# Gathering the first edge tiles from x while the normalized table is made

## The chip, the cores and the metric

The kernel runs on one core of a Trainium2 chip. The metric is the device time of one execution in microseconds, as a median over several runs; lower is better. Engines are named as in the profile: PE is TensorE, DVE is VectorE, ACT is ScalarE, POOL is GpSimd, SP is SyncE (here it only issues transfers).

## The reference

A layer of a graph network is followed by a mixture of experts, in fp32. There are 12500 nodes with 256 features and 212500 edges, sorted by their destination.

```python
f = layernorm(x)                                     # no learned scale
agg = segment_sum(f[src] * edge_weight[:, None], dst, 12500)
x = x + agg @ W.T + b
h = layernorm(x)
e = argmax(softmax(h @ gate_w + gate_b))             # one of 8 experts a token
y = relu(h @ w1[e] + b1[e]) @ w2[e] + b2[e]          # at most 1954 tokens an expert
x = x + nan_to_num(y * probability of e)
```

## The kernel before

**The table.** The first stage normalizes all rows of x and writes them to a table in device memory, `feat`. It runs over LCH: twelve chunks of eight tiles of 128 rows, then one of one tile, then a tail of 84 rows. For each chunk SP loads the rows (`xt`), DVE makes mean and variance (`ln_stats`: L171 and L172), ACT takes one square root for the chunk (L179), DVE inverts and refines it (L182 to L187) and scales the eight tiles (`ln_apply`, L198), and ACT issues the store to `feat` (L161). Two buffers of each kind let a load run ahead.

In the same stage DVE prepares the edges' places: `dst` becomes float, `rel` (the place of each edge's destination in a window of its group), `win` and, for a count of edges that break the windows (`n_bad`), seven more passes over all 1661 columns.

**The main loop.** The edges are cut into KT = 1661 tiles of 128. A loop written out by hand counts steps `s` from 0. In each step one edge tile is gathered, an older one is multiplied, and the other work moves on by one yield:

- `gather(s)` (L628): POOL issues an indirect DMA of 128 rows of `feat` by the indices `src_i[:, s]` into one of 32 buffers `m`.
- `onehot(k + 8)` (L636): DVE makes a weighted one-hot matrix, one of 12 buffers `h`. Here k = s - LEAD and LEAD is 16.
- `product(k)` (L645): PE multiplies it with the gathered rows. Fifteen tiles (a group) add up in one PSUM bank, and ACT copies the sum out (`ws`, L648).
- `fill`: one of 13 writes of 2.57 MB by SP (L223), which preset the pages `buf` of the experts' tokens.
- `nodes()`: for each node tile, the rows of x are loaded on ACT's queue (L669), PE shifts the sums of two to four groups into place (L681), ACT copies (L685), PE multiplies with W (L690), DVE adds x (L693) and makes statistics. After each chunk of eight tiles `ffn.route` normalizes, chooses the expert, and puts the tokens into `buf` (L318, POOL).
- `experts()`: pages of one expert's tokens are loaded, multiplied (L453, L464), finished on DVE and scattered to the output (L495, POOL). Constants count their pace in steps.

Each engine takes its instructions in this written order. A gather waits only for its buffer, so POOL can run up to 32 tiles ahead of the products. A node tile of 128 nodes takes 17 edge tiles. After the last edge tile the rest of the experts follows.

The first gather needs all of `feat`; the stage boundary gives up the first stage's buffers.

Of the kernel before, what the change touches and what calls it, by code (L numbers as in the profile page):

```python
# [9 lines left out]
F32 = mybir.dt.float32  # L10
I32 = mybir.dt.int32
U8 = mybir.dt.uint8
AF = mybir.ActivationFunctionType
ALU = mybir.AluOpType
# [40 lines left out]
AHEAD = 8  # L55
LOADED = 20
PACE = {1: 2.3, 2: 3.0}

# [25 lines left out]
def gnn_moe_kernel(ctx: ExitStack, tc: tile.TileContext, x, src, dst, ew, wT, gb, gate_w, gate_b,  # L86
# [69 lines left out]
    def load_rows(t, src_rows, t0, nt, rows, eng):  # L156
        eng.dma_start(t[:rows, :nt, :],
                      src_rows[t0 * P:t0 * P + nt * rows, :].rearrange("(j p) d -> p j d", p=rows))

    def store_rows(dst_rows, t, t0, nt, rows, eng):  # L160
        return eng.dma_start(  # L161
            dst_rows[t0 * P:t0 * P + nt * rows, :].rearrange("(j p) d -> p j d", p=rows),
            t[:rows, :nt, :])

    def ln_new(pool):
        return pool.tile([P, CH, 6], F32, name="bn"), pool.tile([P, CH, 2], F32, name="mv")

    def ln_stats(ln, x_, j, rows):  # L170
        nc.vector.bn_stats(ln[0][:rows, j, :], x_)  # L171
        nc.vector.bn_aggr(ln[1][:rows, j, :], ln[0][:rows, j, :])  # L172

    def ln_scale(pool, ln, nt, rows):
        v = pool.tile([P, CH], F32, name="ve")
        nc.vector.tensor_scalar_add(v[:rows, :nt], ln[1][:rows, :nt, 1], EPS)
        yield
        s = pool.tile([P, CH], F32, name="sd")
        nc.scalar.activation(s[:rows, :nt], v[:rows, :nt], AF.Sqrt)  # L179
        yield  # L180
        r = pool.tile([P, CH], F32, name="rs")
        nc.vector.reciprocal(r[:rows, :nt], s[:rows, :nt])  # L182
        q = pool.tile([P, CH], F32, name="rq")
        nc.vector.tensor_mul(q[:rows, :nt], r[:rows, :nt], r[:rows, :nt])
        nc.vector.tensor_mul(q[:rows, :nt], q[:rows, :nt], v[:rows, :nt])
        nc.vector.tensor_scalar(q[:rows, :nt], q[:rows, :nt], -0.5, 1.5, op0=ALU.mult, op1=ALU.add)
        nc.vector.tensor_mul(r[:rows, :nt], r[:rows, :nt], q[:rows, :nt])  # L187
        return r

    def through(g):  # L190
        while True:
            try:
                next(g)
            except StopIteration as e:
                return e.value

    def ln_apply(xn, x_, ln, r, j, rows):
        nc.vector.tensor_scalar(xn, x_, ln[1][:rows, j, 0:1], r[:rows, j:j + 1], op0=ALU.subtract,  # L198
                                op1=ALU.mult)
# [345 lines left out]
    with tc.tile_pool(name="edges", bufs=1) as edges:  # L545
# [2 lines left out]
        rel = edges.tile([P, NG * J], F32, name="rel")  # L548
        win = edges.tile([P, NGR], F32, name="win")

        with tc.tile_pool(name="p1", bufs=2) as p1, tc.tile_pool(name="eprep", bufs=1) as ep, \
                tc.tile_pool(name="epsum", bufs=1, space=PSUM) as eps:
            dst_i = ep.tile([P, NG * J], I32, name="dst_i")
            loads = [(dst_i, dst), (src_i, src), (w_sb, ew)]


            for i, (t0, nt, rows) in enumerate(LCH):
                xt = p1.tile([P, CH, D], F32, name="xt")
                load_rows(xt, x, t0, nt, rows, nc.sync)
                if i in (2, 3, 4):  # L560
                    to_sb, of = loads[i - 2]
                    nc.sync.dma_start(to_sb, of.rearrange("p g j -> p (g j)"))
                xn = p1.tile([P, CH, D], F32, name="xn")
                ln = ln_new(p1)
                for j in range(nt):
                    ln_stats(ln, xt[:rows, j, :], j, rows)
                r = through(ln_scale(p1, ln, nt, rows))
                for j in range(nt):
                    ln_apply(xn[:rows, j, :], xt[:rows, j, :], ln, r, j, rows)
                store_rows(feat, xn, t0, nt, rows, nc.scalar)  # L570


            dst_f = ep.tile([P, NG * J], F32, name="dst_f")
            nc.vector.tensor_copy(dst_f, dst_i)
            pb = eps.tile([P, NGR], F32, name="pb")
            nc.tensor.matmul(pb, ones[0:1, :], dst_f[0:1, 0:KT:G], start=True, stop=True)
            base = ep.tile([P, NGR], F32, name="base")
            nc.scalar.copy(base, pb)
            nc.vector.tensor_scalar(win, base, pcol, None, op0=ALU.add)
            line = ep.tile([P, NGR], F32, name="line")  # L580
            nc.gpsimd.iota(line, pattern=[[1, NGR]], base=0, channel_multiplier=0,
                           allow_small_or_imprecise_dtypes=True)
            nc.vector.tensor_scalar(line, line, SLOPE, None, op0=ALU.mult)
            off = ep.tile([P, NG * J], F32, name="off")
            whole = KT // G
            for t, of in ((rel, base), (off, line)):
                a = whole * G
                nc.vector.tensor_sub(t[:, :a].rearrange("p (g j) -> p g j", j=G),
                                     dst_f[:, :a].rearrange("p (g j) -> p g j", j=G),
                                     of[:, :whole, None].to_broadcast([P, whole, G]))  # L590
                if a < KT:
                    nc.vector.tensor_sub(t[:, a:KT], dst_f[:, a:KT],
                                         of[:, whole:whole + 1].to_broadcast([P, KT - a]))
            good = ep.tile([P, NG * J], F32, name="good")
            gv, rv, ov = good[:, :KT], rel[:, :KT], off[:, :KT]
            nc.vector.tensor_scalar(gv, rv, 0.0, None, op0=ALU.is_ge)
            nc.vector.scalar_tensor_tensor(gv, rv, float(P - 1), gv, op0=ALU.is_le, op1=ALU.mult)
            nc.vector.scalar_tensor_tensor(gv, ov, LOW + 0.05, gv, op0=ALU.is_ge, op1=ALU.mult)
            nc.vector.scalar_tensor_tensor(gv, ov, HIGH - 0.05, gv, op0=ALU.is_le, op1=ALU.mult)
            cnt = ep.tile([P, 1], F32, name="cnt")  # L600
            nc.vector.tensor_reduce(cnt, gv, axis=AX.X, op=ALU.add)
            pc = eps.tile([1, 1], F32, name="pc")
            nc.tensor.matmul(pc, ones[:, 0:1], cnt, start=True, stop=True)
            nc.vector.tensor_scalar(n_bad, pc, -1.0, float(P * KT), op0=ALU.mult, op1=ALU.add)

        nc.sync.dma_start(wT_sb, wT.rearrange("(k p) o -> p k o", p=P))
        nc.sync.dma_start(gb_sb, gb.partition_broadcast(P))
        nc.sync.dma_start(gw_sb, gate_w.rearrange("(k p) e -> p k e", p=P))
        nc.sync.dma_start(gateb_sb, gate_b.partition_broadcast(P))

        with tc.tile_pool(name="p2", bufs=32) as p2, tc.tile_pool(name="p2h", bufs=12) as p2h, \
# [11 lines left out]
            def gather(k):  # L626
                m = p2.tile([P, D], F32, name="m")
                nc.gpsimd.indirect_dma_start(  # L628
                    out=m, out_offset=None, in_=feat[:, :],
                    in_offset=bass.IndirectOffsetOnAxis(ap=src_i[:, k:k + 1], axis=0))  # L630
                ffn.before = None
                ms[k] = m

            def onehot(k):
                h = p2h.tile([P, P], F32, name="h")
                nc.vector.tensor_scalar(h, cols, rel[:, k:k + 1], w_sb[:, k:k + 1], op0=ALU.is_equal,  # L636
                                        op1=ALU.mult)
                hs[k] = h
# [81 lines left out]
                            outs.append(ffn.out)  # L720
                    yield

            now, outs = [0], []
            a, b = nodes(), None
            fill = ffn.fill()
            alive = True
            while alive or pages or b or outs:
                s = now[0]
                if s < KT:
                    gather(s)  # L730
                if pool_q:
                    f, j = pool_q.pop(0)
                    f(j)
                else:
                    for o in outs[:1]:
                        if next(o, None) is None:
                            outs.remove(o)
                k = s - LEAD
                if s == 0:
                    for i in range(AHEAD):  # L740
                        onehot(i)
                if 0 <= k < KT:
                    if k + AHEAD < KT:
                        onehot(k + AHEAD)
                    product(k)
                next(fill, None)
                if alive and k >= 0:
                    alive = next(a, 0) is None
                if pages and not b:
                    b = experts(now)  # L750
                if b and next(b, 0) == 0:
                    b = None
                now[0] += 1
# [136 lines left out]
```

## Time and profile before

| | us |
|---|---|
| runs | 3639.66, 3646.94, 3649.23; median 3646.94 |
| profiled execution, its own time | 3609.87 |
| span of the profiled execution | 3607.7 |
| first gather issued (L628, POOL) | 123.86 |
| last gather issued | 3357.6 |
| busy PE / DVE / ACT / POOL | 2035.1 / 1115.3 / 392.2 / 1787.2 |
| mean granted clock of PE | 0.776 |

The profile is one execution of the program. Busy time is the time in which an engine was executing, idle time is put down to whatever ended it, and the DMA share is the mean busy share of the core's 16 DMA engines. Times in the timelines are microseconds from the span's start. A stage table gives, for a stretch of time, the busy time of each engine with its number of instructions. In the operand names, `m<-feat,src_i` is an instruction that writes m and reads feat and src_i.

### The profile page before, as it was taken

What the parts mean: (1) busy time and instruction counts of PE and PEld (TensorE: products, weight loads), DVE (VectorE), ACT (ScalarE), POOL (GpSimd) and SP (SyncE); (2) the same over time, 40 slices, a digit from 0 to 9 for tenths busy, and PEclk for the clock granted to TensorE, in tenths of its full rate; (3) what the DMA queues carried; (4) which work ended last, traced back from release to release, by engine and by line L of the source; (5) the groups of instructions that cost most, each with busy time, mean ns of one, the idle gap of its engine ahead of it and who ended that gap; (6) DMA issues with size and microseconds to landing.
All of it is one profiled execution on the core that took longest, in us unless ns stands there. A gap on an engine that the chain in (4) does not pass through costs nothing. (4 is left out here: it accounts for less than half of the span.)

```text
span 3607.7 us, 30637 instructions
## 1 busy us (share of the span) xinstructions
PE 2035.1 (56%) x9078; PEld 1685.2 (47%) x9078; DVE 1115.3 (31%) x4110; ACT 392.2 (11%) x991; POOL 1787.2 (50%) x1860
## 2 busy tenths in 40 slices
PE   0335536475475475565565557555655646446865
PEld 0134435464364364354455446444444545345765
DVE  8422323232232232322323323222322323323422
ACT  0000000011011011011011011011110101001222
POOL 0466565644654645645545554554555464555200
PEclk9867767786787687787788778777777778678989
DMA  6865333532542533533433343343353252355665
GB/s 235 317 218 185 102 94 94 162 102 81 164 139 73 161 108 110 159 95 124 149 105 117 120 137 106 108 143 98 94 160 118 73 163 72 94 167 172 198 204 174
DMA packets 267818, 495.47 MB, mean 137 GB/s; under 512 B 45027, under 2 KB 162229, under 8 KB 267640
## 3 DMA queue, kind: packets, MB, share of 16 engines
q0 software_dynamic: 91920, 251.53, 22.6%
q1 hardware_dynamic: 136210, 203.42, 17.7%
q10 hardware_dynamic: 39510, 38.41, 3.3%
q8 instruction: 81, 1.33, 0.2%
q14 instruction: 97, 0.79, 0.1%
HBM read 399.69 MB, written 97.44 MB: 138 GB/s over the span
## 5 line engine op out<-in xcount | busy, mean ns | idle before, releaser
L628 POOL DMA_INDIRECT m<-feat,src_i x1661 | 1582.3, 953 | 816.1 <-issue 402.8
L645 PE MATMUL pw<-m,h 128*128 128x256 f32 x3322 | 1010.3, 432 | 250.8 <-DVE h L636 100.2
L645 PEld LDWEIGHTS pw<-m,h 128*128 128x128 f32 x3322 | 686.3, 219 | 386.2 <-issue 244.9
L636 DVE TENSOR_SCALAR h<-cols,rel,w_sb 128x128 f32<-128x128 f32 x1661 | 509.8, 359 | 767.2 <-remote 376.9
L453 PE MATMUL ph<-gT,w_sb 128*128 128x256 f32 (+1 forms) x1856 | 384.3, 360 | 255.9 <-issue 97.3
L453 PEld LDWEIGHTS ph<-gT,w_sb 128*128 128x128 f32 x1856 | 320.0, 208 | 301.6 <-issue 138.9
L495 POOL DMA_INDIRECT out<-z,tok x91 | 92.4, 1015 | 669.3 <-DVE h L636 444.5
L690 PE MATMUL ms<-wT_sb,aT 128*128 128x256 f32 x392 | 137.7, 485 | 445.8 <-ACT aT L685 315.4
L464 PE MATMUL py<-w_sb,hT 128*128 128x256 f32 x1456 | 374.3, 404 | 5.7 <-issue 4.5
L681 PE MATMUL ms<-s,ws 128*128 128x128 f32 x1116 | 197.7, 316 | 301.4 <-issue 196.8
L693 DVE TENSOR_TENSOR rt<-xt,ms 128x256 f32<-128x256 f32 x98 | 41.2, 420 | 1016.6 <-PE ms L690 593.3
L681 PEld LDWEIGHTS ms<-s,ws 128*128 128x128 f32 x1116 | 191.5, 228 | 324.0 <-issue 242.0
L464 PEld LDWEIGHTS py<-w_sb,hT 128*128 128x128 f32 x1456 | 296.5, 207 | 48.7 <-issue 3.7
L690 PEld LDWEIGHTS ms<-wT_sb,aT 128*128 128x128 f32 x392 | 87.9, 236 | 487.1 <-ACT aT L685 336.5
L318 POOL DMA_INDIRECT buf<-rt,to x98 | 111.2, 1135 | 320.4 <-DVE c L347 236.1
L457 ACT ACTIVATE hT<-ph,b_sb 128x256 f32<-128x256 f32 (+1 forms) x464 | 166.8, 426 | 803.8 <-remote 381.4
L256 PE MATMUL ms<-gw_sb,xT 128*128 128x8 f32 x392 | 70.4, 289 | 163.6 <-ACT xT L251 84.4
L256 PEld LDWEIGHTS ms<-gw_sb,xT 128*128 128x128 f32 x392 | 67.1, 239 | 200.3 <-ACT xT L251 118.4
L648 ACT COPY ws<-pw 128x256 f32<-128x256 f32 x111 | 41.2, 371 | 781.5 <-PE pw L645 383.5
L474 DVE TENSOR_TENSOR y<-py,b_sb 128x512 f32<-128x512 f32 (+1 forms) x58 | 33.4, 576 | 290.9 <-PE py L464 265.4
L258 DVE TENSOR_TENSOR lgs<-ms,gateb_sb 128x8 f32<-128x8 f32 x98 | 16.3, 167 | 288.9 <-PE ms L256 138.4
L685 ACT COPY aT<-ms 128x256 f32<-128x256 f32 x98 | 36.4, 372 | 636.1 <-remote 440.5
(143 smaller groups left out, 974.0 us busy)
## 6 DMA issues: line engine op xcount, KB each, us to landing
w_sb<-in_w SPq DMA_DIRECT2D x116, 1024.0 KB
buf<-fill SPq DMA_DIRECT2D x13, 2570.0 KB
m<-feat,src_i POOLq DMA_INDIRECT x1661
pg<-buf SPq DMA_DIRECT2D x33, 514.0 KB
xt<-in_x ACTq DMA_DIRECT2D x97, 128.0 KB
xt<-in_x SPq DMA_DIRECT2D x12, 1024.0 KB
feat<-xn ACTq DMA_DIRECT2D x12, 1024.0 KB
out<-rt ACTq DMA_DIRECT2D x11, 1024.0 KB
```

The costliest lines, as they stand in the source:

```text
L256: nc.tensor.matmul(pl[:rows, :], xT[:, k, :rows], gw_sb[:, k, :], start=(k == 0), stop=(k == 1))
L318: s = nc.gpsimd.indirect_dma_start(out=buf[:, :], out_offset=bass.IndirectOffsetOnAxis(ap=to[:, j, :], axis=0), in_=rt[:rows, j, :], in_of ...
L453: nc.tensor.matmul(ph[:, c:c + n], w1_sb[:, k, f * P:(f + 1) * P], xT[:, k * n:(k + 1) * n], start=(k == 0), stop=(k == 1))
L457: nc.scalar.activation(hT[:, f, :n], ph[:, c:c + n], AF.Relu, bias=b1_sb[:, f:f + 1])
L464: nc.tensor.matmul(py[:, a, :], hT[:, f, a * P:(a + 1) * P], w2_sb[:, f, :], start=(f == 0), stop=(f == F // P - 1))
L495: s = nc.gpsimd.indirect_dma_start(out=out[:, :], out_offset=bass.IndirectOffsetOnAxis(ap=to[:, a, :], axis=0), in_=z[:, a, :], in_offset= ...
L628: nc.gpsimd.indirect_dma_start(out=m, out_offset=None, in_=feat[:, :], in_offset=bass.IndirectOffsetOnAxis(ap=src_i[:, k:k + 1], axis=0))
L636: nc.vector.tensor_scalar(h, cols, rel[:, k:k + 1], w_sb[:, k:k + 1], op0=ALU.is_equal, op1=ALU.mult)
L645: nc.tensor.matmul(product.pw, hs.pop(k), ms.pop(k), start=(j == 0), stop=last)
L648: nc.scalar.copy(ws, product.pw)
L681: nc.tensor.matmul(pa[:, k * P:(k + 1) * P], sums[g][:, k * P:(k + 1) * P], shifts[t, g], start=(g == gs[0]), stop=(g == gs[-1]))
L690: nc.tensor.matmul(px[:rows, :], aT[:, k * P:k * P + rows], wT_sb[:, k, :], start=(k == 0), stop=(k == 1))
```

## The change

The table is no longer a stage of its own. A function `table()` runs inside the main block, before the loop, and does three things in one pass over the chunks:

- It gathers RB = 5 edge tiles in each of its 14 first passes, 70 in all, from `x` itself instead of `feat`. These rows are normalized in place: ACT sums each row (Identity with an accumulator output), a pass later sums the squares of the row minus its mean (Square with a bias and an accumulator output), and a pass after that scales them. The roots and inverses of the five tiles are taken together with those of the chunk's eight (B = 13 columns).
- Of a chunk's eight tiles, ACT scales six (Identity with bias and scale) and DVE two. The inverse of a chunk is taken one pass after its root.
- Four passes after their gather, the five tiles get their one-hots and products. 65 products are done in `table()`; the other five follow in the loop.

The loop then starts at step 70 with `done = made = 65`, and the node tiles may start at once; a product still comes LEAD steps after its gather, so the next one comes at step 81. The edges' places are made in pass 1 (`places()`), and the count `n_bad` is made in the loop's first steps, one DVE pass a step (`check()`). The index list is loaded first; the weights of the node tiles are loaded after the chunks. The buffers of the table are those of the experts' weights (three of each instead of two), which are not in use yet.

The diff, cut to its core:

```diff
+RB = 5
+RAW = RB * len(LCH)
...
             def gather(k):
...
-                    out=m, out_offset=None, in_=feat[:, :],
+                    out=m, out_offset=None, in_=x[:, :] if k < RAW else feat[:, :],
...
+            def table():
+                nc.sync.dma_start(src_i, src.rearrange("p g j -> p (g j)"))
...
+                for i in range(n + 3):
+                    if i < n:
+                        t0, nt, rows = LCH[i]
+                        xts[i] = p4.tile([P, CH, D], F32, name="xt", tag="w1_sb", bufs=3)
+                        load_rows(xts[i], x, t0, nt, rows, nc.sync)
+                        for k in range(i * RB, (i + 1) * RB):
+                            gather(k)
...
+                    if 0 <= i - 1 < n:
+                        batch[i - 1] = p3.tile([P, 2, RB], F32, name="sums", bufs=3)
+                        for j in range(RB):
+                            junk = p3.tile([P, D], F32, name="junk", bufs=1)
+                            nc.scalar.activation(junk, ms[(i - 1) * RB + j], AF.Identity,
+                                                 accum_out=batch[i - 1][:, 0, j:j + 1])
+                    if 0 <= i - 2 < n:
+                        sq[i - 2] = p3.tile([P, RB], F32, name="squares")
+                        for j in range(RB):
+                            junk = p3.tile([P, D], F32, name="junk", bufs=1)
+                            nc.scalar.activation(junk, ms[(i - 2) * RB + j], AF.Square,
+                                                 bias=batch[i - 2][:, 1, j:j + 1],
+                                                 accum_out=sq[i - 2][:, j:j + 1])
+                    if i >= 1:
+                        r = ln_inverse(p3, vs[i - 1], ss[i - 1], B, P)
...
+                        for j in range(nt):
+                            if j % 4 == 3:
+                                ln_apply(xn[:rows, j, :], xt[:rows, j, :], lns[i - 1], r, j, rows)
+                            else:
+                                nc.scalar.activation(xn[:rows, j, :], xt[:rows, j, :], AF.Identity,
+                                                     bias=nb[:rows, j:j + 1], scale=r[:rows, j:j + 1])
+                        store_rows(feat, xn, t0, nt, rows, nc.scalar)
+                    if 0 <= i - 3 < n:
+                        for j in range(RB):
+                            m = ms[(i - 3) * RB + j]
+                            nc.scalar.activation(m, m, AF.Identity, bias=nb[:, CH + j:CH + j + 1],
+                                                 scale=r[:, CH + j:CH + j + 1])
+                    if i == 1:
+                        places()
...
+                        for j in range(nt):
+                            ln_stats(lns[i], xts[i][:rows, j, :], j, rows)
...
+                    ss[i] = ln_root(p3, vs[i], B, P)
+                    if i >= 4:
+                        for k in range((i - 4) * RB, (i - 3) * RB):
+                            onehot(k)
+                            product(k)
...
-            now, outs = [0], []
+            done = table()
+            made = done
+            now, outs = [RAW], []
...
-            fill = ffn.fill()
+            extra = [ffn.fill(), check()]
...
-                k = s - LEAD
-                if s == 0:
-                    for i in range(AHEAD):
-                        onehot(i)
-                if 0 <= k < KT:
-                    if k + AHEAD < KT:
-                        onehot(k + AHEAD)
-                    product(k)
-                next(fill, None)
-                if alive and k >= 0:
+                while made < min(KT, max(done, s - LEAD) + AHEAD):
+                    onehot(made)
+                    made += 1
+                if done < KT and done <= s - LEAD:
+                    product(done)
+                    done += 1
+                for e in extra:
+                    next(e, None)
+                if alive:
```

## The prediction

> **What bounds the kernel now.** I read, in this order, the page, the stage table (busy time of each engine in stretches that I chose), the same table for the gathered tile m alone, the timelines of the table stage, and the ScalarE groups by form. The chain that ended last covers only the last scatter here and says nothing on the stages, so stages carry the argument. All engines by stretch, columns PE, PEld, DVE, ACT, POOL, clock, DMA share, GB/s:
>
> ```profile
> 0.00:123.80 123.80, 0.95 (x4) 0.58 (x4) 99.86 (x415) 4.35 (x16) 1.34 (x10) 1.00 0.69 234
> 123.80:221.00 97.20, 42.19 (x115) 24.95 (x116) 21.00 (x67) 1.49 (x4) 66.60 (x70) 0.72 0.82 297
> 414.00:3358.00 2944.00, 1717.89 (x7483) 1422.26 (x7482) 865.45 (x3129) 309.96 (x742) 1581.35 (x1636) 0.76 0.39 121
> ```
>
> The first 123.8 us make the table: VectorE is busy 81%, ScalarE 3.5%, POOL and TensorE do nothing. The next 97.2 us hold the first 70 gathers (POOL x70), so a gather costs 1.39 us there. In the long stage no engine is over 59%: the engines wait for each other along the written order of steps. Its 1471 gathers (m alone) make 2.00 us a gather, and nothing in the diff touches one of those steps. The two ends of the first 70 gathers, on POOL:
>
> ```profile
> 123.86 1.15 POOL L628 DMA_INDIRECT m<-feat,src_i  x1 [121.93 <-DVE h L636]
> ...
> 221.04 0.94 POOL L628 DMA_INDIRECT m<-feat,src_i  x1 [0.30 <-issue]
> ```
>
> The first waits 121.93 us for the table; the second is gather 70, the first that the changed kernel still takes from feat. How a chunk of the table runs (timeline):
>
> ```profile
> 90.07 2.67 DVE L198 TENSOR_SCALAR xn<-xt,mv,rs 128x256 f32<-128x256 f32 x8
> 92.72 0.75 DVE L171 BATCH_NORM_STATS2 bn<-xt 128x6 f32<-128x256 f32 x2
> 92.78 0.46 ACTq L161 DMA_DIRECT2D feat<-xn  x1
> ...
> 97.63 2.67 DVE L198 TENSOR_SCALAR xn<-xt,mv,rs 128x256 f32<-128x256 f32 x8
> ...
> 100.33 0.46 ACTq L161 DMA_DIRECT2D feat<-xn  x1
> ```
>
> A chunk takes 100.33 - 92.78 = 7.55 us, VectorE without a pause: 3.2 statistics, 1.7 the root and its inverse, 2.67 scaling.
>
> **What the skill says.** "ScalarE: Activation LUTs", What ACT_TABLE_LOAD costs: an ACTIVATE takes 186 ns + 0.833 ns an element, about 93 ns more for each per-partition pointer operand, and back-to-back ones overlap by 93 ns. The ScalarE groups agree:
>
> ```profile
> L477 ACT ACTIVATE y<-y,pg 128x256 f32<-128x256 f32 x91 | 42.6, 503 | 307.6 <-DVE y L474 242.7 <-issue 61.3 <-DMA w_sb<-in_w 3.6
> L179 ACT ACTIVATE sd<-ve 128x8 f32<-128x8 f32 x23 | 4.8, 209 | 128.4 <-DVE ve L176 113.4 <-issue 5.8 <-DVE h L636 2.9
> ```
>
> One pointer, 256 elements: the page's sum is 492, measured 503. "ScalarE activation tables: per-element evaluation and per-set limits", What a function is on this engine: the accumulator output adds results into the engine's accumulator. No price is given, and the kernel before has no such instruction. "DMA: Bandwidth & Descriptors", Queues, rings and completion order: each DMA engine goes round-robin between the queue rows with work. That fits 124 to 209 us, where fill writes and gathers share the engines (DMA share 0.85, 311 GB/s), POOL issues 62 gathers, but only 31 products (62 rows of m) run.
>
> **The change, part by part.**
>
> ScalarE in one full pass of the new table loop: five sums, no pointer, 399 - 93 = 306 ns by the page; five squares with a pointer bias, 492 - 93 = 399; six table scalings and five in-place scalings of m with two pointers, 585 - 93 = 492 each; the store's issue 0.46 (above); the root 0.21 and about 0.1 for its wait. The accumulator's read-out is unknown: no cost (lower bound) to one more small ACTIVATE plus the lost overlap, 0.209 + 0.093 = 0.30 us (upper). It can hardly be a gain, since work is added. I take 0.19. Sum: 5 x 0.50 + 5 x 0.59 + 11 x 0.49 + 0.77 = 11.6 us a pass; 9.7 and 12.7 at the bounds.
>
> Others in that pass: VectorE 3.2 statistics, 0.7 for two scalings, 1.3 inverse with its wait, 0.9 for five small ops, 1.5 for five one-hots = 7.6. POOL 5 x 1.25 (the steps of its timeline) = 6.3. DMA: 1.05 MB load, 1.05 store, 0.66 gathers = 2.75 MB, at the 281 GB/s of 60 to 100 us 9.8 us, at the 337 of 150 to 200 us 8.2. So ScalarE becomes the bound, with DMA close behind; that is why a free read-out buys little below 9.7. Square must not swap the table against Sqrt: a swap is 1.28 us by the ACT_TABLE_LOAD row. The page says cheap functions come in every set and gives square the budget of identity; I take none.
>
> The table's length: the source list now loads first, so the first root is at about 13 us (11.5 before). Pass 1 holds six scalings, and on VectorE the 4.2 us of places() (cast 1.0, rel 1.87, the matmul and copy between): to 24.5. Pass 2, 16 ACTIVATEs: to 34. Ten passes of 11.6: to 150. Pass 13, one table tile: 9.1, to 159. Pass 14 to its store: 6.5, to 165.7. Before, the last store's issue at 121.11 let the gather go at 123.86, 2.75 us later. Gather 70 starts at **168.5 us**, against 221.0: 52 us earlier. Passes 15 and 16 (8 us more on ScalarE) run beside it: POOL may be 32 buffers ahead of the products. The 65 products, 65 x 0.86 us, lie where TensorE was idle.
>
> What moves with it. The fills now begin at step 70 and slow gathers 70 to 140 as they slowed 0 to 70: both streams go through the same stretch, 70 gathers further on, so it cancels. Six VectorE passes of check() (10.4 us) move from a bound stage into steps 70 to 77, where no product is due before step 81: hidden. The three node loads that ScalarE issued early at 47 us, and the four weight loads from SP, now come at the table's end: 1.4 us of issue and a landing beside the fills, about 4 us, partly under the late gathers. I charge 4 in all: net **-48 us**.
>
> On the profiled execution's own time, 3609.87 (span 3607.7), this gives 3562; that execution lies 37 us under the median of the runs, 3646.94. The step is taken off the median: **3599 us**.
>
> **Rivals.**
>
> (1) Light ScalarE: the read-out is free, a pass is 9.7, DMA-bound too. Ten passes save 19 us more: gather 70 at 149.5, 3580. For it: the page has no price. Against: five results must leave an accumulator one by one.
>
> (2) Heavy ScalarE: each accumulating ACTIVATE must also wait for the one before (all write the same junk tile) and costs 0.35 above the 0.19. A pass is 15.1, gather 70 comes at 204, the gain is 17 - 4 = 13 us: 3634. At 17 us a pass it is gone.
>
> (3) Slower: the fills come too late for the first scatters. SP issued 13 fills over 193 us, and from 214 us on they follow the node loads (SP, then ScalarE's queue):
>
> ```profile
> 214.07 104.60 SPq L223 DMA_DIRECT2D buf<-fill  x6
> ```
> ```profile
> 211.86 0.37 ACTq L669 DMA_DIRECT2D xt<-in_x  x1
> 233.36 0.34 ACTq L669 DMA_DIRECT2D xt<-in_x  x1
> 254.86 0.33 ACTq L669 DMA_DIRECT2D xt<-in_x  x1
> ```
>
> The queues share completion semaphores, so fills wait for a load that comes once per node tile, 21.5 us apart. The last landed near 326 (318.3 and about 8); the first scatter into buf ran at 414.3 and waited for its own addresses. Shifted, the scatter is wanted at 414 - 52 = 362; the fills start 43 us later and end at 369. That is 7 us late at the old pace; but with node tiles 0 to 2 now ready at step 70 their loads come sooner, so I count none. If three more fills fall behind node loads, they end at 369 + 65 = 434: 72 us late, POOL stands on the scatter with all later gathers queued behind it, and 72 - 48 = 24 us are lost: 3671. It decides from two and a half more.
>
> (4) The change doesn't do what it says: the long stage gives back what the start won, because something not in the gather stream paces it. Against: groups of sums, node tiles and pages are all counted in gathers. No change, 3647.
>
> **How the numbers follow.** Forecast 0.62 (own range 3580 to 3618), rival 1 0.13, rival 2 0.12, rival 3 0.09, rival 4 0.04. A measurement of this kernel can tell about 0.3%, 11 us, from no change. Faster: 0.62 + 0.13 + most of rival 2 (0.10) = 0.85; same: 0.02 + 0.04 = 0.06; slower 0.09. The range runs from under rival 1 (3565) to past rival 2 (3638).
>
> **What would show it.** Right: ScalarE nearly full from 25 to 160 us, passes of 11 to 12 us between store issues, the first gather within 10 us of the start, gather 70 at 160 to 180, the long stage still at 2.0 us a gather. Wrong: store issues 9.7 apart (rival 1) or 14 and more (2); ACT_TABLE_LOADs in the table stage; a scatter into buf waiting for buf<-fill (3); more than 2.02 us a gather in the long stage (4).

## The result and the profile after

The changed kernel takes 3608.34 us, median of 5 runs (3603.12 to 3608.53), against 3646.94 for the kernel before (3632.55 to 3649.23) in the same comparison: 38.6 us less, a ratio of 0.990 with the 95% interval 0.988 to 0.9921. The forecast was 3599; its step of 48 us was 9 us too large. The profiled execution of the changed kernel is 3603.12 us, its span 3601.3, at a mean clock of 0.760.

The stage table of the changed kernel, cut at gather 70, at gather 140, and at the first put into `buf` and the last gather (columns PE, PEld, DVE, ACT, POOL, clock, DMA share, GB/s):

```profile
0.00:184.00 184.00, 47.34 (x108) 33.64 (x109) 97.64 (x443) 144.59 (x422) 69.56 (x79) 0.75 0.61 206
184.00:287.30 103.30, 55.17 (x194) 41.72 (x193) 41.55 (x125) 12.14 (x34) 72.28 (x71) 0.70 0.94 337
376.60:3348.50 2971.90, 1712.64 (x7483) 1425.45 (x7483) 858.09 (x3132) 310.42 (x741) 1578.96 (x1636) 0.75 0.40 120
```

In the table's stretch ScalarE is now the busiest engine, 144.59 of 184 us, where it had 4.35 of 123.8; POOL issues 70 gathers in it (x79 with its other work). The long stage holds the same 7483 matmuls and 1636 POOL instructions, and nearly the same busy times, as before. Its 1400 gathers from number 200 to 1600 take 2.00 us each (before: 1.99).

The two ends of the 70 raw gathers on POOL:

```profile
5.64 1.12 POOL L579 DMA_INDIRECT m<-in_x,src_i  x1 [3.90 <-DMA src_i<-in_src]
...
184.05 0.94 POOL L579 DMA_INDIRECT m<-feat,src_i  x1 [30.22 <-PE pw L596]
```

The first gather now waits only for the index list. Gather 70 starts at 184.05 instead of 221.04: **37.0 us earlier**. (It is put down to a product, but the product that frees its buffer, number 38 in pass 11, ended at 152.7, some 31 us earlier; the last store to `feat` was issued at 181.4, 2.6 us before.) In what follows, the *lead* is the time by which the changed kernel starts a gather earlier than the kernel before starts the same one. It stays near 37 us through most of the stream: 35.3 us at gather 140, 37.6 at 200, 38.0 at 500, 41.3 at 1400, 36.5 at 1520.

One pass of the table on ScalarE, from store to store:

```profile
90.35 0.47 ACTq L165 DMA_DIRECT2D feat<-xn  x1
90.86 2.58 ACT L771 ACTIVATE m<-m,nb,rs 128x256 f32<-128x256 f32 x5 [0.54 <-ACT xn L765]
93.35 0.20 ACT L180 ACTIVATE sd<-ve 128x13 f32<-128x13 f32 x1
...
93.70 0.42 ACT L743 ACTIVATE junk<-m 128x256 f32<-128x256 f32 x1
94.02 0.19 ACT L743 ACTIVATION_READ_ACCUMULATOR junk<-m 128x1 f32 x1
94.25 0.42 ACT L743 ACTIVATE junk<-m 128x256 f32<-128x256 f32 x1
...
96.42 0.51 ACT L749 ACTIVATE junk<-m,sums 128x256 f32<-128x256 f32 x1
96.83 0.19 ACT L749 ACTIVATION_READ_ACCUMULATOR junk<-m,sums 128x1 f32 x1
97.06 0.51 ACT L749 ACTIVATE junk<-m,sums 128x256 f32<-128x256 f32 x1
...
99.48 3.06 ACT L765 ACTIVATE xn<-xt,nb,rs 128x256 f32<-128x256 f32 x6
102.56 0.46 ACTq L165 DMA_DIRECT2D feat<-xn  x1
```

It is full: 102.56 - 90.35 = 12.2 us, and the only idle time is the 0.54 us of the store's issue (this pass also holds one group's sum copy; the passes without one take 11.9). Each sum or square is two instructions, the ACTIVATE and a read-out of the accumulator. From start to start, a sum comes every 0.54 us, a square every 0.64, a scaling every 0.49.

One pass of this execution was different. Pass 3 took 17.7 us. From 41 to 51 us ScalarE and VectorE both paused between instructions, without waiting for each other (`<-issue` and `<-remote` mean that the profile shows no instruction or transfer of this program that ended the wait):

```profile
43.19 0.51 ACT L749 ACTIVATE junk<-m,sums 128x256 f32<-128x256 f32 x1 [1.59 <-remote]
43.61 0.19 ACT L749 ACTIVATION_READ_ACCUMULATOR junk<-m,sums 128x1 f32 x1
46.01 0.51 ACT L749 ACTIVATE junk<-m,sums 128x256 f32<-128x256 f32 x1 [2.21 <-issue]
```

This and the end of the stream were the open points. In this pair of profiles the lead falls from 36.5 us at gather 1520 to 9.1 at gather 1660, and the spans differ by 6.4 us only (3607.7 and 3601.3), while the medians differ by 38.6.

### The profile page after: what moved, and what is told of

It reads as the page before. It is cut to its first block, busy times and chain, and to the rows that moved or that the text cites. A ratio compares the mean times of both kernels' runs of the same rounds, so it can differ in the third digit from the quotient of the medians.

```text
span 3601.3 us, 31128 instructions
## 1 busy us (share of the span) xinstructions
PE 2053.0 (57%) x9078; PEld 1708.6 (47%) x9078; DVE 1101.0 (31%) x4115; ACT 541.5 (15%) x1418; POOL 1792.6 (50%) x1859
## 3 DMA queue, kind: packets, MB, share of 16 engines
q8 instruction: 81, 1.33, 0.2%
## 5 line engine op out<-in xcount | busy, mean ns | idle before, releaser
L579 POOL DMA_INDIRECT m<-feat,src_i x1591 | 1520.3, 956 | 729.3 <-issue 387.4
L596 PE MATMUL pw<-m,h 128*128 128x256 f32 x3322 | 1021.6, 438 | 253.1 <-DVE h L587 135.6
L596 PEld LDWEIGHTS pw<-m,h 128*128 128x128 f32 x3322 | 699.6, 223 | 381.3 <-issue 217.3
L587 DVE TENSOR_SCALAR h<-cols,rel,w_sb 128x128 f32<-128x128 f32 x1661 | 499.9, 354 | 729.0 <-remote 349.9
L632 PE MATMUL ms<-s,ws 128*128 128x128 f32 x1116 | 207.2, 324 | 411.2 <-ACT ws L599 256.1
L599 ACT COPY ws<-pw 128x256 f32<-128x256 f32 x111 | 41.3, 372 | 661.0 <-remote 311.5
L579 POOL DMA_INDIRECT m<-in_x,src_i x70 | 68.4, 977 | 83.7 <-PE pw L596 63.6
```

The source lines that it names most:

```text
L579: nc.gpsimd.indirect_dma_start(out=m, out_offset=None, in_=x[:, :] if k < RAW else feat[:, :], in_offset=bass.IndirectOffsetOnAxis(ap=src_ ...
L596: nc.tensor.matmul(product.pw, hs.pop(k), ms.pop(k), start=(j == 0), stop=last)
L599: nc.scalar.copy(ws, product.pw)
L632: nc.tensor.matmul(pa[:, k * P:(k + 1) * P], sums[g][:, k * P:(k + 1) * P], shifts[t, g], start=(g == gs[0]), stop=(g == gs[-1]))
```

## The experiments

**Theory.** The gain is the lead: the time at which the kernel before starts gather RAW, less the time at which the table ends. The rest of the stream carries it nearly unchanged. The table's length is its passes on the engine that is fullest, here ScalarE. **Rivals.** The gain comes from the faster table alone, or goes with the number of raw tiles, or the two engines wait for each other and no single one bounds a pass.

The experiments ran on three chips, on all of which the stream goes at 1.41 to 1.42 us a gather and the kernel before takes 2698 to 2701 us. Where the pair above ran is not recorded, and why it was slower there stays open. The traces show in what the slowness consists. In the two profiles of the pair VectorE stands 111 and 96 times for more than 1.5 us, 842 and 740 us in all, and TensorE 70 and 66 times, in waits that end by `issue` or `remote`. In the ten profiles of the experiments neither engine has one such wait. Each gain below is against runs of the kernel before on the same chip. "Lead" is the start of a gather against the same gather in e1, the one profile of the kernel before on these chips.

| run | table's end: first gather from feat | lead there | lead at gather 200 | gain in the medians | ratio, 95% |
|---|---|---|---|---|---|
| e2 no raw tiles | 0 at 103.3 (before 125.8) | 22.5 | 17.5 | 18.1 | 0.991 to 0.9942 |
| e3 RB = 3 | 42 at 134.0 (178.8) | 44.8 | 40.0 | 38.7 | 0.9823 to 0.9862 |
| e5 the change, RB = 5 | 70 at 175.2 (213.9) | 38.6 | 33.6 | 32.5 | 0.9848 to 0.989 |
| e4 scaling on VectorE | 70 at 151.7 | 62.2 | 57.1 | 54.4 | 0.9772 to 0.9805 |
| e6 e4, products early | 70 at 151.2 | 62.7 | 57.1 | 62.3 | 0.975 to 0.9791 |
| e7 statistics on VectorE | 70 at 132.6 | 81.2 | 76.0 | 72.9 | 0.9706 to 0.9741 |
| e8 e7, RB = 7 | 98 at 145.6 (249.1) | 103.5 | 81.1 | 78.7 | 0.9682 to 0.9723 |
| e9 e5, check() in the table | 70 at 177.8 | 36.1 | 35.7 | 37.6 | 0.9843 to 0.9884 |
| e10 e8, fills early | 98 at 150.8 | 98.3 | 91.9 | 92.5 | 0.9641 to 0.967 |

In all nine the gain is the lead at gather 200 within 5 us or so. From gather 500 to gather 1400 all nine leads shrink by 2.0 to 5.8 us against this one profile of e1; no run tells whether that belongs to the change or to e1's execution.

### e1: the kernel before, once more

> The kernel before, unchanged, for a profile on the same chip as the runs below. In the pair of profiles so far gather 70 starts 37 us earlier after the change and gather 1520 still 36.5 us earlier, but the spans differ by 6.4 us only. Theory A: the lost 30 us belong to the chip on which the profile of before was taken (granted clock 0.776 against 0.760): this run's own time is near 3640, its clock near 0.76, and its gather 1600 starts some 30 us later than in the old profile. Theory B: the change itself gives 30 us back at the end of the stream: this run's last gathers stand where they stood in the old profile (1660 at 3357), and its time is near 3610.

It took 2699.46 us at a clock of 0.866, far from both numbers, and the question of the pair's last 100 gathers is not answered by this run itself. It gives the base of the table above. The making of the table takes as long as in the first profile (last store issued at 123.1 us, 121.1 in the first profile); only what follows is quicker.

### e2: no raw tiles

```diff
-RAW = RB * len(LCH)
+RAW = 0
...
-             B = CH + RB
+             B = CH
```

The gathers, sums, squares and scalings of m in `table()` go with it, and the loop starts at step 0.

> The change without its gathers from x: the table alone, with six of eight scalings on ScalarE, inverse a pass late, places in pass 1, then the stream from step 0. Theory A: the gain is the time of gather RAW in the kernel before, less the end of the table. Without raw gathers a pass is bound by its transfers (2.1 MB at 281 to 337 GB/s, 6.2 to 7.5 us) and by VectorE (about 6.5), so the last store is out at about 108 us, the first gather at 105 to 112 against 123.6: gain 12 to 18 us, time about 3625 to 3635. Rival: the gain comes from the faster table and not from the raw tiles: this kernel keeps all of the 38 us, about 3608.

Measured: passes of 6.6 us, the first gather at 103.3 us, gain 18.1 us. The faster table alone gives less than half of what e3 gives, so the rival falls as the whole cause. But it is a large part: 18.1 us is more than half of the 32.5 that the change itself gains (e5). The raw tiles as the change makes them add only the other 14. In the stage table of 36 to 95 us VectorE has 87% and the DMA share is 0.94:

```profile
36.00:95.00 59.00, 0.00 (x0) 0.00 (x0) 51.23 (x222) 29.13 (x63) 0.00 (x0) 1.00 0.94 306
```

The waits tell the two apart. VectorE never waits for a load there, only for the root, so it bounds the pass:

```profile
DVE rs L185 <- ACT sd L180: 2.5, 9, 0.3
```

(us in total, times, the longest.)

### e3: three raw tiles a pass

```diff
-RB = 5
+RB = 3
```

> RB = 3 in place of 5: 42 raw tiles. A pass of ScalarE takes 12.0 - 2 x (0.54 + 0.64 + 0.51) = 8.6 us. Theory A (gain = the time that gather RAW had before, less the end of the table): the table ends 11 passes x 3.4 = 37 us sooner, gather 42 at about 143 us; in the kernel before, gather 42 started at about 177, so the gain is about 34 to 38 us, as much as with 70 tiles: 3603 to 3613. ScalarE's cost of a raw tile in time (13 x 1.69 = 22 us for each one of RB) is then about what a raw tile is worth (14 gathers x 1.39 us = 19 us). Rival: the gain goes with the number of raw tiles: 3/5 of 38 = 23 us, 3624.

Measured: most passes at 8.6 us, as worked out, gather 42 at 134.0, gain 38.7 us. 42 raw tiles bring at least as much as the 70 of e5: the number of tiles is not what counts. A tile more in RB costs ScalarE (11.9 - 8.6) / 2 = 1.67 us a pass, 14 x 1.67 = 23 us in all, and moves 14 gathers of 1.26 us = 18 us out of the stream.

### e4: all of the table's scaling on VectorE

```diff
-                            if j % 4 == 3:
+                            if j >= 0:
                                 ln_apply(xn[:rows, j, :], xt[:rows, j, :], lns[i - 1], r, j, rows)
```

> All eight scalings of a chunk on VectorE, the rest as in the change. Theory A (ScalarE is the bound of a pass): ScalarE falls from 12.0 to 12.0 - 6 x 0.51 = 8.9 us, VectorE rises from 7.6 to 7.6 + 6 x 0.35 = 9.7 to 10.5; a pass takes about 10.5 and gather 70 starts at about 165 us in place of 184: 15 to 20 us faster than the change, 3589 to 3595. Rival: a pass is bound by the order of the two engines (each waits for the other once a pass), and moving work buys nothing or costs: gather 70 at 184 or later, 3608 to 3620.

Measured: gather 70 at 151.7, a median 54.4 us below that of the kernel before, where the change has 32.5. ScalarE was the bound, and work taken off it shortens the table. The passes were uneven: most 8.3 to 9.8 us, but two of 14.8 and 14.2. In those ScalarE stood on the copy of a group's sum:

```profile
72.44 0.21 ACT L180 ACTIVATE sd<-ve 128x13 f32<-128x13 f32 x1 [1.42 <-DVE ve L794]
77.29 0.37 ACT L599 COPY ws<-pw 128x256 f32<-128x256 f32 x1 [4.63 <-PE pw L596]
77.56 0.42 ACT L743 ACTIVATE junk<-m 128x256 f32<-128x256 f32 x1
```

The copy waits 4.63 us for the fifteenth product, and the next pass's sums are queued behind it. Is that order the stall, or does it only show that VectorE is late?

### e5: the change once more

> The change itself once more, for a second profile. Open is the stretch from 41 to 51 us of its first profile, in which ScalarE and VectorE both paused 1.3 to 2.3 us between instructions and pass 3 took 17.8 us instead of 12.0. Theory A: a single event of that execution; pass 3 now takes 12 us, gather 70 starts at about 176 us. Theory B: it belongs to the kernel (first full pass with gathers, load and store at once); pass 3 takes 16 us or more again and gather 70 starts at 183 to 185. By the rule that the time gained is the lead of gather 70 over the kernel before on the same chip, less the 5 to 8 us that the runs e3 and e4 lost behind it: on a chip where gather 70 of before starts at 214, A gives a gain of 30 to 33 us and B of 22 to 25; where it starts at 221, 37 to 40 and 29 to 32.

The pause did not come back: pass 3 took 9.7 us, the next ones 11.9 to 12.2, and gather 70 started at 175.2. So the kernel does not make the pause, as theory A had it; 184.0 against 175.2, it cost some 8 to 9 us. Whether it came in one execution only or in all of the first runs is not shown: waits of its kind fill both profiles of the pair, and no later one has them. What it was stays open. The lead at the end stays too: 28.5 us at gather 1520, 28.7 at 1660. So the change need not lose its lead in the last 100 gathers; why the first pair of profiles does stays open.

Early in the stream the lead falls once, by 5 us, between gathers 70 and 97. POOL's timeline and VectorE's, at that place:

```profile
186.57 1.32 POOL L579 DMA_INDIRECT m<-feat,src_i  x1 [0.30 <-issue]
188.20 2.33 POOL L579 DMA_INDIRECT m<-feat,src_i  x1 [0.30 <-DMA m<-feat,src_i]
190.83 2.32 POOL L579 DMA_INDIRECT m<-feat,src_i  x1 [0.30 <-PE ms L632]
193.46 1.62 POOL L579 DMA_INDIRECT m<-feat,src_i  x1 [0.30 <-issue]
195.38 2.08 POOL L579 DMA_INDIRECT m<-feat,src_i  x1 [0.30 <-PE ms L632]
197.76 0.95 POOL L579 DMA_INDIRECT m<-feat,src_i  x1 [0.31 <-issue]
```
```profile
186.53 0.49 DVE L230 MEMSET fill<- 128x514 f32 x1
...
187.12 1.88 DVE L681 TENSOR_TENSOR off<-dst_f,line 128x1650 f32<-128x1650 f32 x1
...
189.39 1.02 DVE L705 TENSOR_SCALAR good<-rel 128x1661 f32<-128x1661 f32 x1
190.44 1.89 DVE L709 SCALAR_TENSOR_TENSOR good<-rel,good 128x1661 f32<-128x1661 f32 x1
192.37 1.89 DVE L709 SCALAR_TENSOR_TENSOR good<-off,good 128x1661 f32<-128x1661 f32 x1
...
194.76 1.89 DVE L709 SCALAR_TENSOR_TENSOR good<-off,good 128x1661 f32<-128x1661 f32 x1
```

Nobody waits, the idle column is 0.30 throughout: the gathers themselves take longer, while check() runs its wide passes (six over all columns, not seven as said of the kernel before). At this point that is a coincidence in time, since the fills start at the same step.

### e6: products ahead of the statistics

```diff
                     if i == 1:
                         places()
+                    if i >= 4:
+                        for k in range((i - 4) * RB, (i - 3) * RB):
+                            onehot(k)
+                            product(k)
```

(and the same lines taken away behind the root; all else as e4)

> As e4 (all eight scalings on VectorE), and the one-hots and products of a pass stand ahead of its statistics instead of behind them. In e4 three of the passes took 9.8 to 14.9 us instead of 8.3 to 9: there the copy of a group's sum (ws) stands in ScalarE's order ahead of the next pass's sums and waited 4.0 to 4.6 us for the fifteenth product, whose one-hot VectorE makes at the end of its pass. Theory A (that order is the stall): the products run beside the statistics, the copy finds them done, all passes take 8.3 to 9 us, gather 70 starts at about 140 us against 151.7, and the time falls about 11 us below e4: 2633 on the chip of e4. Rival: VectorE is the bound of those passes and the wait only shows it: gather 70 stays at about 150, no gain over e4.

The two long passes are gone, and the passes in the middle of the table all take 10.1 to 10.2 us; gather 70 comes at 151.2, as in e4. So the rival holds: the stall only showed that VectorE was behind. A long pass of e4 and the two behind it average (14.2 + 8.3 + 8.9) / 3 = 10.5, near the same. The stage tables of e4 and of e6, 42 to 120 us:

```profile
42.00:120.00 78.00, 29.45 (x70) 21.51 (x70) 69.92 (x294) 61.67 (x200) 35.08 (x38) 0.70 0.83 264
```
```profile
42.00:120.00 78.00, 32.44 (x71) 22.53 (x72) 72.09 (x300) 63.70 (x206) 37.19 (x40) 0.62 0.82 271
```

VectorE has 90% and 92%, ScalarE 79% and 82%. The median is 8 us below e4's, but the intervals overlap and the leads at gather 200 are equal, so no gain is claimed.

### e7: the raw tiles' statistics on VectorE

```diff
-                            nc.scalar.activation(junk, ms[(i - 1) * RB + j], AF.Identity,
-                                                 accum_out=batch[i - 1][:, 0, j:j + 1])
...
+                        todo += [(ms[(i - 1) * RB + j], CH + j, P) for j in range(RB)]
...
+                    for x_, j, rows in todo:
+                        nc.vector.bn_stats(bn[:rows, j, :], x_)
+                    for x_, j, rows in todo:
+                        nc.vector.bn_aggr(mv[:rows, j, :], bn[:rows, j, :])
```

(all thirteen scalings on ScalarE; a raw tile is ready one pass sooner)

> The raw tiles' statistics on VectorE (bn_stats and bn_aggr, all bn_stats of a pass first) in place of the accumulating sums and squares; all scalings on ScalarE; products early as in e6. ScalarE: 13 x 0.51 + 0.9 = 7.5 us a pass. VectorE: 13 statistics at 0.53 = 6.9, inverse and nb 1.5, one-hots 1.4, 0.2 more: 10.0 at most, perhaps 9 since the pairs no longer wait for each other. Theory A (the longer of the two engines sets the pass): passes of 9 to 10 us, gather 70 at 142 to 150 us; gain over before 57 to 65 us less than e6 by nothing to 8. Rival: transfers set it (2.75 MB a pass at 281 to 337 GB/s: 8.2 to 9.8 us), then e6 and this kernel have equal passes, and the wait ahead of statistics is for m or xt.

Measured: passes of 8.8 us, gather 70 at 132.6, gain 72.9 us: better than expected, and better than e6, which theory A had not foreseen. One bn_stats and one bn_aggr replace two accumulating ACTIVATEs with their read-outs, so work is taken away and not only moved. The order pays as well: issued in two runs, bn_stats starts every 0.33 us and bn_aggr every 0.07, 0.39 us a tile, where the alternating pairs of e2 and of the change take 0.53. Since the scalings moved too, what each of the three is worth is not shown apart. The rival, transfers, falls: from 42 to 120 us VectorE waits for no load and no gather, only for the root:

```profile
DVE rs L185 <- ACT sd L180: 7.1, 9, 1.0
```

### e8: seven raw tiles a pass

```diff
-RB = 5
+RB = 7
```

> As e7 with RB = 7, 98 raw tiles. VectorE: 15 statistics 8.0, inverse 1.5, one-hots 1.9, 0.2: 11.6 us a pass at most; ScalarE 8.6. Theory A (gain = lead of gather RAW over before): gather 98 at 155 to 168 us; in before on the chip of e1 it starts at 249, so 81 to 94 us of lead and, less 5 to 8, a gain of 73 to 89: faster than e6 and e7. Each further tile of RB costs 14 x 0.8 = 11 us of VectorE and is worth 14 x 1.27 = 18 us of gathers. Rival: the transfers of a pass (3.0 MB, 9 to 11 us) already set it and POOL's 32 buffers (three passes of 7 are 21, four are 28) hold the gathers back, so that a pass takes 13 us or more and nothing is gained over e7.

Passes took 9.7 us, gather 98 came at 145.6, the lead was 103.5 us: more than expected. Of that only 81.1 was left at gather 200, and the gain of 78.7 us is not clear of e7's 72.9, as the two intervals overlap. About 5 us went to check(), as in e5, and the rest in one place, the first put into `buf`, on POOL:

```profile
264.89 0.95 POOL L579 DMA_INDIRECT m<-feat,src_i  x1 [0.30 <-PE ms L641]
283.58 1.01 POOL L329 DMA_INDIRECT buf<-rt,to  x1 [17.74 <-issue]
```

The last of the 13 fills was issued at 255.8. This is rival 3 of the prediction, which the change itself did not meet: its first put came at 376.6, 83 us after its last fill was issued.

### e9: check() in the table

```diff
+                    if i in (6, 7, 8):
+                        for _ in range(2 if i < 8 else 4):
+                            next(extra[1], None)
```

> The change with its check() moved from the loop's first steps into passes 6 to 8 of the table (two or three of its DVE passes in each). In e5 five gathers took 1.32, 2.33, 2.32, 1.62 and 2.08 us of POOL instead of 0.95, just while VectorE ran the wide passes of check() (186.9 to 196.6 us), 4.9 us in all, and the lead over before fell from 38.6 us at gather 70 to 33.6 at gather 97. Theory A (the wide passes on VectorE slow the gathers on POOL): in the table POOL has spare time, the passes stay at 12.0 us since VectorE has over 4 us free in each, the lead at gather 97 stays at 38, and the gain over before rises from 32.5 to about 37 us. Rival: the gathers were slowed by the fills that start at the same step, not by check(): then five gathers beside the fills' start are as long as before, and the lead falls to 33 again.

The lead is 36.1 us at gather 70 and 35.9 at gather 97. Beside the fills' start only one gather is long, while VectorE sets the 514 columns of `fill`:

```profile
189.05 1.33 POOL L579 DMA_INDIRECT m<-feat,src_i  x1 [0.30 <-PE pw L596]
```

So theory A holds and the fills slow nothing there: gathers 70 to 97 take 1.26 us each. Part of the 5 us was paid elsewhere: soon after check(), which puts two wide passes in each of passes 6 to 8, one pass took 14.6 us where e5 has 12.2 (the copy of a group's sum stood 2.33 us for a product), and gather 70 came 2.5 us later than in e5. The gain in the medians, 37.6 against 32.5, points the same way, but the intervals overlap; the traces decide.

### e10: the fills early

```diff
+                    if i >= n:
+                        for _ in range(3):
+                            next(extra[0], None)
```

(and the four weight loads in front of it)

> As e8 (RB = 7), with the weights' loads and six of the 13 fills issued in passes 14 and 15 of the table instead of in the loop. In e8 the first scatter into buf stood on POOL for 17.7 us until 283.6 us, with the last fill issued at 255.8, and the lead over before fell from 98.5 to 81 us. Theory A (the scatter waits for the fills): the fills start near 132 us instead of 153.5, so they end some 15 to 20 us sooner; the scatter goes at 266 to 270, its wait is 5 us or less, and the time falls 12 to 17 us below e8, to some 2603 to 2607 where before takes 2698. Rival: from the table's end to that scatter the DMA engines are full (363 GB/s, share 0.99 in e8), so fills that start sooner only slow the last stores and the gathers beside them; gather 98 then starts later than 150 us, and the time stays within 5 us of e8.

```profile
271.54 0.94 POOL L579 DMA_INDIRECT m<-feat,src_i  x1 [0.30 <-DMA buf<-fill]
272.79 1.01 POOL L329 DMA_INDIRECT buf<-rt,to  x1 [0.30 <-DVE bn L175]
```

The put no longer waits, and comes 11 us sooner. The rival has its share: gather 98 starts 5.2 us later than in e8, because the last stores now land beside fills (it starts 7.6 us after the last store's issue, in e8 2.6; from 145 to 151 us 335 GB/s move, in e8 67). All in all it is a gain of 92.5 us over before, 3.4%, the best version found.

## Why the prediction was right, and which steps were off

**The mechanism** was right: the lead at gather 70 goes through the stream, apart from what is said of check() below. The first pair shows it to gather 1520, the experiments to the end. **Rival 4** falls.

**The pass** of 11.6 us was 11.9, with ScalarE its bound (e3, e4). From start to start the sums took 0.54 us (0.50 in the forecast) and the squares 0.64 (0.59); the scalings, at 0.49, were as taken, and the rest was less. The unknown read-out, taken as 0.19 between 0 and 0.30, lengthens a sum to 0.54 from the prediction's estimate of 0.306 without one: 0.24. **Rivals 1 and 2** fall with it: the steady passes were neither 9.7 nor 15.1, and the shared junk tile made no wait beyond it.

**The table's length** was mis-sized. By e5, free of the pause: root 1 at 27.7 us, not 24.5; ten passes from root 2 to root 12 in 119.5, not 116; pass 13 9.6, not 9.1; its store and the landing as worked out. Together gather 70 at 175.2, not 168.5. The 3.2 us at the start are a wait that the sum left out: in `places()` the copy of `base` stands in ScalarE's order behind the six scalings of pass 1, and VectorE stood 4.6 us for it:

```profile
21.13 1.88 DVE L681 TENSOR_TENSOR rel<-dst_f,base 128x1650 f32<-128x1650 f32 x1 [4.57 <-ACT base L692]
```

In the profiled execution the pause of some 8 to 9 us comes on top: 184.05. So the lead there was 37, not 52.

**"check() is hidden"** was wrong. It costs 5 us (e5, e9; e2 to e8 each lose 4.3 to 5.0 us soon behind the table), and not through a late product, which was the only path considered. "SBUF — State Buffer", Who interferes with whom, in the Trainium skill says that a VectorE instruction with two inputs in SBUF contends with a GpSimd instruction that reads SBUF. The traces agree: in e5 gathers that start inside one of the two-input passes of 1.88 us take 1.62 to 2.33 us instead of 0.95, and the one-input reduction of 1.85 us behind them stretched none. The sentence does not cover all of it: the comparison of 1.02 us and the setting of `fill` lengthen a gather too (last section). In the first pair the same gathers are stretched:

```profile
200.75 3.11 POOL L579 DMA_INDIRECT m<-feat,src_i  x1 [0.30 <-remote]
```

But there the lead fell only from 37.0 to 36.4 us, because POOL in the kernel before also stood twice for some 3 us in these gathers (`<-remote`). The 4 us charged for something else, weight and node loads beside the fills, thus came near check()'s cost on the later chips by chance; in the pair nothing was lost. **"The fills cancel"** was right (e9: 1.26 us a gather beside them, as for gathers 0 to 70 in e1).

**One reading of the profile before** is not borne out. The prediction took the 31 products of 124 to 209 us as a sign that fills and gathers share the DMA engines. TensorE stood 32 us in that stretch for nothing that the profile shows, and in e1, with the same fills and more bytes moved, 62 products run in as long a time. The waiting instruction, then the work on the gathered tile m, before and e1 (PE, PEld, POOL, clock, DMA share, GB/s):

```profile
208.67 0.80 PE L681 MATMUL ms<-s,ws 128*128 128x128 f32 x2 [32.06 <-issue]
```
```profile
124.00:209.00 85.00, 29.43 (x62) 13.54 (x62) 58.43 (x62) 0.71 0.85 311
126.00:211.00 85.00, 52.28 (x124) 24.90 (x124) 64.59 (x68) 0.85 1.02 373
```

POOL stood in waits of the same kind, so the 221 us from which the lead was counted are long too: in e1 gather 70 starts at 213.9.

**Rival 3** did not come in the change, where fills were issued in 94 us instead of 193, and the put waited for addresses. It is real: at RB = 7 it took 17.7 us.

**The numbers.** Forecast 48 us, medians 38.6, interval 0.79% to 1.2% or 29 to 44 us. In the pair the table ended 15.5 us later than forecast, by e5 6.7 of them mis-sized terms and 8.8 the pause; that leaves 37.0 of 52.5, and the 4 us charged behind it were not lost. That the lead in this one pair of executions agrees with the medians is in part luck: both executions held such waits, and that of the kernel before took 3609.87 us, 37 below its median, so the two spans differ by 6.4 us only. The experiments, whose profiles have no such pauses, carry the account: 38.6 us of lead at gather 70, 5 lost to check(), 32.5 gained.

## What to carry to other kernels

When a stream is only delayed by a stage, the gain of starting it early is the time at which it would have come to the same item, less the time at which the stage now ends; each item taken early is worth its own pace and costs its work on the fullest engine, so price the two against each other before choosing how many. Make the variant without the early items, too: here the faster stage alone was more than half of the gain. Moving work to an idle engine helps until that engine is the fullest; the version that also did the work in fewer and better ordered instructions gained more. And before calling a wide VectorE pass hidden, look at what POOL is doing in that time, not only at who waits for the result.

## What was not expected of the hardware

An ACTIVATE with an accumulator output shows as two instructions. With the read-out of 188 ns the next sum starts 0.24 us later than the prediction's estimate for an ACTIVATE without one:

```profile
L743 ACT ACTIVATION_READ_ACCUMULATOR junk<-m 128x1 f32 x70 | 13.2, 188 | 0.0
```

How long a gather is stretched depends on where in the VectorE pass it starts. One that starts inside a two-input pass of 1.88 us ends 0.81 to 0.83 us behind the pass. This holds for all 39 such gathers in the twelve profiles, leaving out those that also meet the comparison named below the table:

| run | two-input pass on VectorE | gather starts | pass still to run | gather takes |
|---|---|---|---|---|
| e5 | 190.44 to 192.33 | 190.83 | 1.50 | 2.32 |
| e5 | 194.76 to 196.65 | 195.38 | 1.27 | 2.08 |
| e5 | 192.37 to 194.26 | 193.46 | 0.80 | 1.62 |
| e10 | 18.92 to 20.80 | 20.06 | 0.74 | 1.56 |
| e10 | 18.92 to 20.80 | 18.81, ahead of the pass | 1.88 | 0.94 |

The comparison with one input (`good<-rel`), 1.02 us, also holds up a gather that is already running: in e9 it ends at 84.25, and the gather beside it at 84.37, after 2.59 us. The setting of `fill` with 0.44 us to run made one of 1.33.

The same kernel before took 3647 us in the first runs and 2698 to 2701 on the chips of the experiments, with the table's stage alike (123.9 and 125.8 us to the first gather) and the stream at 1.99 and 1.41 us a gather, at clocks of 0.776 and 0.866. The long waits of VectorE and TensorE for nothing that the profile shows are in the first two profiles alone; no run tells why.
